# A graph layer with a mixture of experts: scatter the expert outputs to rows of their own and add them on TensorE, instead of accumulating them by DMA

## The chip, the cores and the metric

The kernel runs on one core of a Trainium2 chip. The metric is the device time of one execution in microseconds (us), the median of several runs. All data are float32 unless said.

## The reference, cut to what matters

```python
# x: 12500 x 256; src, dst: 212500 edges, sorted by dst; 64 experts, two for each node
h = x * rsqrt(deg_out)[:, None]
m = segment_sum(h[src], dst) * rsqrt(deg_in)[:, None]
x1 = (m @ W_gc + b_gc) + (x @ W_res + b_res)
vals, idx = top_k(x1 @ Wg + bg, 2);  gates = softmax(vals)
core = sum over a node's two experts e of  gate_e * (gelu(x1 @ w1[e] + b1[e]) @ w2[e] + b2[e])
y = x1 + core                                  # 256 -> 512 -> 256 in each expert
y = (y - mean over nodes) * rsqrt(var over nodes + eps) * gamma + beta
out = layernorm(x + y)                         # along the 256 features
```

The change touches how `core` of a part of the nodes is summed over the two experts of a node, and brought into `y`.

## The kernel before

**Nodes and stages.** The 12500 nodes are 98 tiles of 128 (the last has 84). Tiles 0 to 43 (`TA = 44`, 5632 nodes) are called the earlier nodes here, tiles 44 to 97 (6868 nodes) the later ones. By the trace, the stages are: loads and degrees, to 133 us; the edge stage, to about 2320, in which POOL gathers 128 rows of `h_d` at a time by indirect DMA (L766, 1596 of them) and PE sums them by destination with a one-hot matmul (L783), and in which the experts already work on the earlier nodes; some 30 us of tables; the expert stage for the later nodes, 2350 to 3032; the tail, which ends at 3163.

**The earlier nodes** have their experts' outputs in a DRAM tensor `oa_d`, in expert order. They are collected in the expert stage of the later nodes (below).

**The expert stage of the later nodes** (from L1675). The 64 experts come in descending order of their number of rows, each with room for a fixed number of rows (`TOKENS_B`, in units of 32), one part each: the first parts have four tiles of up to 128 rows, later ones two, the last ones one; 142 tiles in all. For each part:

- weights `w` and `bb` are loaded by SP (L1685, L1687), three buffers each;
- POOL gathers the part's node rows, one indirect DMA a tile, `xg` (L1695, 13 buffers), three parts ahead;
- PE transposes them (L1710), DVE copies them to `xT` (L1714);
- PE multiplies with the first weight (L1723), ACT applies gelu (L1727), PE multiplies with the second (L1750);
- DVE adds the bias and scales with the gate, into `yo` (L1755, L1760; 6 buffers);
- POOL scatters the 128 rows of `yo` by an indirect DMA to the DRAM tensor `z_d` (L1761), with `compute_op=ALU.add`: the DMA adds onto what the row holds. `z_d` has one row for each later node, and 1024 spare rows for empty slots.

A row of `z_d` gets two additions, from two experts. So `z_d` is zeroed ahead, by 31 DMAs of 256 KB on SP in the edge stage (L1629), and the scatters of different experts are ordered by semaphores: an expert's first scatter waits until the previous expert's last has landed. Scatters of one expert are declared independent (`group=f"expert{i}"`, "no node has an expert twice").

**Beside parts 0 to 43** one tile of the earlier nodes is collected a part: `brought` loads four tiles of `cy` from DRAM on SP (L1776) at every fourth part; `added` issues two gathers a tile on POOL from `oa_d` (`co`, L1785, 6 buffers), and DVE adds each with its gate onto `cy` (L1791); after each four, `turned_nodes` transposes them on PE (L1801), with `bn_stats` on DVE (L1802) and a copy on ACT (L1803) into `acc2`, which holds all nodes transposed (feature by node). The order on each engine is the order of the code: for part q the first matmuls, gathers for part q+3, transposes of part q+1, second matmuls and scatters of part q, then the collecting.

**The tail** (from L1913). SP loads `z_d` (L1926) into `zt`, in units of eight tiles (1 MB; the first has four, the last two one each), four buffers. `acc2` holds the later nodes' `x1` rows, not yet transposed. For the first four tiles of a unit DVE adds `zt` to them (L1930) and PE transposes the sum (L1943); for the other four PE transposes (L1945) and adds `zt` by a matmul with the identity that accumulates in the same PSUM (L1948). Then `bn_stats` on DVE (L1954) and a copy back on ACT (L1956). The first load waits for every scatter. Behind the loads, on SP, stands a prefetch of x (L1966, `z<-in_x`, six loads). When the last statistics are there, a short chain on DVE makes mean and variance over all nodes, and the final stage scales, transposes back (L2024, L2025), adds x, does the layer norm and stores.

Of the kernel before, what the change touches and what calls it, by code (L numbers as in the profile page):

```python
# [88 lines left out]
NA = TA * P  # L89
TOKENS_A = [  # L90
# [18 lines left out]
NODES_B = [(TA, 4)] + [(t, 8) for t in range(TA + 4, 96, 8)] + [(96, 1), (97, 1)]  # L109
# [30 lines left out]
def gnn_moe_kernel(  # L140
# [33 lines left out]
    z_d = dram.tile([NP - NA + 4 * 2 * P, D], F32, name="z_d")  # L174
# [1448 lines left out]
    z_all = z_d.rearrange("(a p r) d -> a p (r d)", p=P, r=2)  # L1623
    with tc.manual_schedule(engines=EVERY):
        fetch(0)
        for i in range(4):
            at_row(CA + 4 + 20 * i, lambda t, i=i: cleared([3 + i, NPW - 4 + i]))
        for i in range((NT - TA) // 2 + 4):
            at_row(CA + 90 + 12 * i, lambda t, i=i: nc.sync.dma_start(  # L1629
                z_all[i], acc_d[0][:, : 2 * D]  # L1630
            ))
        nodes_go[0] = True
        begin_nodes(CA)
        go(CA, MC)
# [10 lines left out]
    )  # L1645
    held = one.tile([P, NSLOT], F32)
# [11 lines left out]
    V.tensor_scalar_add(rank, rank, float(N - NA))  # L1658
    V.scalar_tensor_tensor(rank, held, 0.0, rank, op0=ALU.is_equal, op1=ALU.mult)
    V.tensor_tensor(slot[:, 1], rank, slot[:, 0], op=ALU.add)  # L1660
# [13 lines left out]
    with ExitStack() as stack:  # L1674
# [83 lines left out]
        def outputs(w, bb, at, gate, h1, m, group):  # L1758
            for k, r, yo in products(w, bb, h1, m):
                V.tensor_scalar_mul(yo[:r], yo[:r], gate[:r, k : k + 1])  # L1760
                st = GP.indirect_dma_start(  # L1761
                    out=z_d,
                    out_offset=bass.IndirectOffsetOnAxis(ap=at[:r, k : k + 1], axis=0),
                    in_=yo[:r],
                    in_offset=None,
                    compute_op=ALU.add,
                )
                if group:
                    tc.declare_no_dep(st.ins, group=group, reason="no node has an expert twice")
                    tc.add_to_no_dep_group(group, st.ins)  # L1770
# [79 lines left out]
        for q, (i, b, m) in enumerate(parts):  # L1850
            h1 = hidden(given[i][0], xT, m)
            if q + AHEAD < len(parts):
                begin(q + AHEAD)
            if q + 1 < len(parts):
                xT = turned(q + 1)
            outputs(*given[i], table(q, 1), gate.pop(q), h1, m, f"expert{i}")
            if q < TA:
                u, k = divmod(q, 4)
                if k == 0:
                    ys[u] = brought(u)  # L1860
                added(ys[u], pos_a[:, :, u * 4 : u * 4 + 4], k)
                if k == 3:
                    turned_nodes(ys[u], u)

        with tc.If(nc.values_load(over_n[0:1, 0:1]) > 0):
# [25 lines left out]
            for a in range(NT - TA):  # L1891
                nc.sync.dma_start(z_d[a * P : (a + 1) * P], none)
            with tc.For_i(0, E, 1) as e:
# [5 lines left out]
                for b in range(0, RPE, 4):  # L1899
                    g = gather(at[:, 0, b : b + 4], 4)  # L1900
                    gb = gates_of(g, second[:, b : b + 4])
                    outputs(w, bb, at[:, 1, b : b + 4], gb, hidden(w, turn(g), 4 * P), 4 * P, None)

    with ExitStack() as stack:
# [14 lines left out]
        z3 = z_d[: NP - NA].rearrange("(t p) d -> p t d", p=P)  # L1919
# [3 lines left out]
        for t0, n in [(t, n) for t, n in NODES_B]:  # L1923
            r = rows(t0)
            zt = zq.tile([P, 8, D], F32, name="zt")
            nc.sync.dma_start(zt[:r, :n], z3[:r, t0 - TA : t0 - TA + n])  # L1926

            m = min(n, 4)
            y = acc2[:r, :, t0 * P : (t0 + m) * P].rearrange("p h (t d) -> p t h d", d=P)
            V.tensor_add(y, y, zt[:r, :m].rearrange("p t (h d) -> p t h d", h=2))  # L1930
            if t0 == 96:
                continue
            for b in range(0, n, 4) if t0 < 96 else [-1]:
                for h in range(2):
                    q = ps2.tile([P, 4, P], F32, name="q")
                    at = 0
                    for i in range(4):
                        t = t0 + b + i
                        if t < NT:
                            r = rows(t)  # L1940
                            y = acc2[:r, h, t * P : (t + 1) * P]
                            if b < 4:
                                T.transpose(q[:, i, :r], y, ident[:r, :r])  # L1943
                            else:
                                T.matmul(  # L1945
                                    q[:, i], y, ident, start=True, stop=False, is_transpose=True
                                )
                                T.matmul(  # L1948
                                    q[:, i], zt[:, b + i, h * P : (h + 1) * P], ident,
                                    start=False, stop=True,  # L1950
                                )
                            at += r
                    q = q.rearrange("p a b -> p (a b)")[:, :at]
                    V.bn_stats(stat[:, h, (t0 + b) // 4], q)  # L1954

                    S.copy(acc2[:, h, (t0 + b) * P : (t0 + b) * P + at], q)  # L1956
# [148 lines left out]
```

## Time and profile before

| | us |
|---|---|
| median of 3 runs (lowest, highest) | 3160.55 (3154.66, 3164.33) |
| the profiled execution, its span | 3165.16, 3163.4 |
| busy in the span: PE, DVE, POOL, ACT | 2501.8, 1645.8, 2145.9, 728.5 |
| expert stage, parts 0 to 43 (2387 to 2860) | 473: PE busy 387.35, POOL 340.93 |
| last 16 scatters, from 2941 on | POOL busy 24.7 |
| PE's last expert matmul ends, first tail load | 3000.06, 3032.01 |
| first matmul of the final stage (L2024) | 3068.52 |

How to read it: PE is TensorE's matmuls and PEld its weight loads, DVE VectorE, ACT ScalarE, POOL GpSimd, SP SyncE (only DMA issues here). In the groups a row is line, engine, operation, out<-in, count, then busy time and mean ns of one, then the idle time just before them with what ended it. In the timelines a row is start, duration, engine, line, operation, and in brackets the idle time before it and its releaser. "issue" is time in which the engine waited for nothing that the profile shows. Releasers are inferred: where the engine that is named had long been done, it was something else. The granted clock of TensorE is 1.00 at full speed.

### The profile page before, as it was taken

The page shows a single profiled execution, that of the slowest core. Times are in us where ns is not written, and L with a number is a line of the kernel's source. Part 1 is how long each engine was busy: PE and PEld are TensorE (multiplying, and loading weights), DVE is VectorE, ACT ScalarE, POOL GpSimd, SP SyncE. Part 2 cuts the span into 40 slices and gives each one's busy share as a digit, 9 for nine tenths or more (in the row PEclk, how much of TensorE's full clock was granted, in tenths as well). Part 3 has the DMA queues.
Part 4 walks back from the last instruction along what each step waited for, and adds up shares of the span by engine and source line. Part 5 has one row for each costly group of instructions (what it writes and reads, how often), then busy time and mean ns, then how long its engine had stood idle before and what let it go on. Part 6 is the DMA issues. An engine that isn't in the chain of part 4 may idle for free. (4 is left out here: it accounts for less than half of the span.)

```text
span 3163.4 us, 41525 instructions
## 1 busy us (share of the span) xinstructions
PE 2501.8 (79%) x12664; PEld 1847.1 (58%) x12733; DVE 1645.8 (52%) x6067; ACT 728.5 (23%) x2126; POOL 2145.9 (68%) x2113
## 2 busy tenths in 40 slices
PE   2477777778788887898999989898958988679755
PEld 1244445544565654766777667677735666567655
DVE  8477765552487774553444343344554433334257
ACT  2022333330111111222221122122201112112246
POOL 0677777777777777777777777777747767666200
PEclk9889988996899998999999999999979999889878
DMA  8733333333665555666667677778746767778658
GB/s 285 241 96 101 102 105 104 109 114 113 207 182 164 159 164 162 184 187 189 198 193 207 201 207 209 204 232 256 230 128 154 179 174 197 182 205 227 203 156 269
DMA packets 297179, 567.59 MB, mean 179 GB/s; under 512 B 56921, under 2 KB 203493, under 8 KB 288753
## 3 DMA queue, kind: packets, MB, share of 16 engines
q0 software_dynamic: 110912, 271.07, 32.3%
q1 hardware_dynamic: 172325, 280.68, 28.4%
q10 hardware_dynamic: 13708, 13.06, 1.3%
q8 instruction: 105, 1.72, 0.2%
q14 instruction: 129, 1.06, 0.1%
HBM read 496.86 MB, written 75.89 MB: 181 GB/s over the span
## 5 line engine op out<-in xcount | busy, mean ns | idle before, releaser
L766 POOL DMA_INDIRECT ring<-h_d,src_col x1596 | 1575.6, 987 | 577.4 <-issue 427.8
L783 PE MATMUL p<-ring,o 128*128 128x257 f32 (+1 forms) x3192 | 1061.0, 434 | 316.4 <-DMA ring<-h_d,src_col 281.3
L783 PEld LDWEIGHTS p<-ring,o 128*128 128x128 f32 x3192 | 565.5, 205 | 548.7 <-DMA ring<-h_d,src_col 337.7
L758 DVE TENSOR_SCALAR o<-lane,rel 128x128 f32<-128x128 f32 x1596 | 399.7, 297 | 230.1 <-PE p L783 229.1
L1761 POOL DMA_INDIRECT z_d<-yo,tables x142 | 222.1, 1564 | 158.7 <-DVE yo L1755 65.2
L1750 PE MATMUL yp<-w,h 128*128 128x256 f32 (+3 forms) x1136 | 273.5, 392 | 39.0 <-DVE yo L1755 39.0
L1282 ACT ACTIVATE acc<-p,acc 128x128 f32<-128x128 f32 (+4 forms) x332 | 128.1, 386 | 736.0 <-PE p L1271 445.1
L236 DVE TENSOR_TENSOR acc<-bank,acc 125x2450 bf16<-125x2450 bf16 (+1 forms) x136 | 185.1, 1361 | 198.5 <-PE bank L1458 189.5
L1723 PE MATMUL hp<-xT,w 128*128 128x128 f32 (+12 forms) x1024 | 239.5, 389 | 60.4 <-DVE xT L1714 59.8
L1306 DVE TENSOR_TENSOR acc<-yp_a,acc 128x256 f32<-128x256 f32 (+3 forms) x120 | 50.1, 418 | 420.3 <-PE yp_a L1299 417.2
L1750 PEld LDWEIGHTS yp<-w,h 128*128 128x128 f32 (+3 forms) x1136 | 193.6, 178 | 96.7 <-DVE yo L1755 44.7
L1723 PEld LDWEIGHTS hp<-xT,w 128*128 128x128 f32 x1024 | 181.1, 205 | 112.2 <-DVE xT L1714 63.8
L1271 PE MATMUL p<-acc 128*128 128x128 f32 (+4 forms) x1328 | 238.0, 302 | 4.4 <-ACT s L818 0.6
L1271 PEld LDWEIGHTS p<-acc 128*128 128x128 f32 x1328 | 209.3, 193 | 47.1 <-ACT acc L1282 25.7
L1299 PE MATMUL yp_a<-acc 128*128 128x256 f32 (+3 forms) x960 | 235.6, 390 | 0.0
L1727 ACT ACTIVATE h<-hp,w 128x128 f32<-128x128 f32 (+12 forms) x256 | 117.0, 459 | 480.9 <-PE hp L1723 419.8
L1453 ACT ACTIVATE acc<-lane_b,acc 125x128 bf16<-125x128 bf16 x544 | 168.2, 389 | 240.8 <-PE bank L1462 149.5
L1299 PEld LDWEIGHTS yp_a<-acc 128*128 128x128 f32 (+3 forms) x960 | 162.9, 174 | 47.4 <-issue 9.6
L1695 POOL DMA_INDIRECT xg<-xb_d,tables x142 | 139.8, 985 | 44.3 <-issue 21.9
L818 ACT COPY s<-p 128x257 f32<-128x257 f32 (+1 forms) x133 | 49.6, 373 | 502.3 <-PE p L783 402.1
L1458 PEld LDWEIGHTS <-acc 125*128 125x128 bf16 x1156 | 88.4, 106 | 105.2 <-issue 62.5
L1235 POOL DMA_INDIRECT acc<-xa_d,tables x120 | 116.9, 974 | 36.5 <-issue 30.5
(349 smaller groups left out, 3122.6 us busy)
## 6 DMA issues: line engine op xcount, KB each, us to landing
w<-in_wpack SPq DMA_DIRECT2D x64, 1026.0 KB
acc<-in_wpack SPq DMA_DIRECT2D x128, 512.0 KB
ring<-h_d,src_col POOLq DMA_INDIRECT x1596
tables<-h_d SPq DMA_DIRECT2D x105, 128.0 KB
acc<-acc_d SPq DMA_DIRECT2D x14, 896.0 KB
xt<-in_x ACTq DMA_DIRECT2D x48, 256.0 KB
z<-in_x SPq DMA_DIRECT2D x12, 1024.0 KB
out<-z SPq DMA_DIRECT2D x11, 1024.0 KB
```

Source lines behind the costliest of these rows:

```text
L236: V.tensor_tensor(o.rearrange("p k (a b) -> p k a b", b=2), lane_b[:p, None, :n] .rearrange("p k (a b) -> p k a b", b=2) .to_broadcast([p, ...
L758: o_last[u] = V.tensor_scalar(o_of[u][:, j], lane, rel[:, c : c + 1], None, op0=ALU.is_equal)
L766: i = GP.indirect_dma_start(out=r[:, k, :D], out_offset=None, in_=h_d, in_offset=bass.IndirectOffsetOnAxis(ap=src_col[:, c : c + 1], axis=0),)
L783: i = T.matmul(p_of[g][:, :n], o_of[v][:, m], r[:, k, :n], start=j == 0, stop=j == GR - 1)
L1271: T.matmul(hp, w1[:, c, j * P : (j + 1) * P], xT[:, c, :m], start=c == 0, stop=c == 1,)
L1282: S.activation(h1[:, j, :m], hp_of.pop((q, j)), AF.Gelu, bias=b1_a[i % 2][:, j : j + 1])
L1299: T.matmul(y, h1[:, j, k * P : k * P + n], w2[:, j], start=j == 0, stop=j == 3)
L1453: S.activation(s_los[k % 2][:, j], lane_b[:EP], AF.Sign, bias=nbs[u % 2][:, i, j : j + 1])
L1695: GP.indirect_dma_start(out=g, out_offset=None, in_=of, in_offset=bass.IndirectOffsetOnAxis(ap=at[:, k : k + 1], axis=0),)
L1723: T.matmul(hp[:, :m], w1[:, c, j * P : (j + 1) * P], xT[:, c, :m], start=c == 0, stop=c == 1,)
L1750: T.matmul(yp[:r], h1[:, j, k * P : k * P + r], w2[:, j], start=j == 0, stop=j == 3,)
L1761: st = GP.indirect_dma_start(out=z_d, out_offset=bass.IndirectOffsetOnAxis(ap=at[:r, k : k + 1], axis=0), in_=yo[:r], in_offset=None, comp ...
```

## The change

`z_d` gets two planes of `ZR = NP - NA` rows, one for a node's first expert and one for its second (`second` is 1 where the slot holds the node's second expert), and behind them one spare row for every slot that can be empty. No row is written twice, so the scatter writes plainly, nothing is zeroed, and all scatters are in one group without dependences. In the tail each unit is four tiles, loaded from both planes by two DMAs of 512 KB; PE transposes the `x1` rows and accumulates both planes by two matmuls with the identity. Only the last two tiles are added on DVE.

```diff
+ZR = NP - NA
-NODES_B = [(TA, 4)] + [(t, 8) for t in range(TA + 4, 96, 8)] + [(96, 1), (97, 1)]
+NODES_B = [(t, 4) for t in range(TA, 96, 4)] + [(96, 1), (97, 1)]
-    z_d = dram.tile([NP - NA + 4 * 2 * P, D], F32, name="z_d")
+    z_d = dram.tile([2 * ZR + E * CAP, D], F32, name="z_d")
-        for i in range((NT - TA) // 2 + 4):
-            at_row(CA + 90 + 12 * i, lambda t, i=i: nc.sync.dma_start(
-                z_all[i], acc_d[0][:, : 2 * D]
-            ))
+    to = one.tile([P, NSLOT], F32)
+    GP.iota(
+        to, pattern=[[CAP, E], [P, RPE]], base=2 * ZR, channel_multiplier=1,
+        allow_small_or_imprecise_dtypes=True,
+    )
-    V.tensor_scalar_add(rank, rank, float(N - NA))
-    V.scalar_tensor_tensor(rank, held, 0.0, rank, op0=ALU.is_equal, op1=ALU.mult)
-    V.tensor_tensor(slot[:, 1], rank, slot[:, 0], op=ALU.add)
+    V.scalar_tensor_tensor(to, held, 0.0, to, op0=ALU.is_equal, op1=ALU.mult)
+    V.scalar_tensor_tensor(to, second, float(ZR), to, op0=ALU.mult, op1=ALU.add)
+    V.tensor_tensor(slot[:, 1], to, slot[:, 0], op=ALU.add)
...
                     in_=yo[:r],
                     in_offset=None,
-                    compute_op=ALU.add,
                 )
-                if group:
-                    tc.declare_no_dep(st.ins, group=group, reason="no node has an expert twice")
-                    tc.add_to_no_dep_group(group, st.ins)
+                tc.declare_no_dep(st.ins, group="z", reason="a row of its own for each output")
+                tc.add_to_no_dep_group("z", st.ins)
...
+        z4 = z_d[: 2 * ZR].rearrange("(k t p) d -> p k t d", p=P, k=2)
...
+            zt = zq.tile([P, 2, 4, D], F32, name="zt")
+            for k in range(2):
+                nc.sync.dma_start(zt[:r, k, :n], z4[:r, k, t0 - TA : t0 - TA + n])
+            if n == 1:
+                y = acc2[:r, :, t0 * P : (t0 + 1) * P]
+                for k in range(2):
+                    V.tensor_add(y, y, zt[:r, k, 0].rearrange("p (h d) -> p h d", h=2))
...
+                    else:
+                        T.matmul(q[:, i], y, ident, start=True, stop=False, is_transpose=True)
+                        for k in range(2):
+                            T.matmul(
+                                q[:, i], zt[:, k, i, h * P : (h + 1) * P], ident,
+                                start=False, stop=k == 1,
+                            )
```

On POOL, at the end of the expert stage, the last scatters with what each waits for (a DMASW name is the semaphore of one of eight slots for POOL's DMAs; a wait on its own slot is a matter of counting, the second one is the previous expert's last scatter). Before:

```order
L1761 DMA z_d<-yo,tables 7936x256 [waits DMASW3_49,DVE_49] x2
L1761 DMA z_d<-yo,tables 7936x256 [waits DMASW5_49,DVE_49]
L1761 DMA z_d<-yo,tables 7936x256 [waits DMASW6_49,DMASW5_49,DVE_49]
L1761 DMA z_d<-yo,tables 7936x256 [waits DMASW7_49,DMASW6_49,DVE_49]
L1761 DMA z_d<-yo,tables 7936x256 [waits DMASW7_49,DVE_49]
L1761 DMA z_d<-yo,tables 7936x256 [waits DMASW1_49,DMASW0_49,DVE_49]
```

The same place in the changed kernel:

```order
L1762 DMA z_d<-yo,tables 79360x256 [waits DMASW2_49,DVE_49]
L1762 DMA z_d<-yo,tables 79360x256 [waits DMASW3_49,DVE_49]
L1762 DMA z_d<-yo,tables 79360x256 [waits DMASW4_49,DVE_49]
L1762 DMA z_d<-yo,tables 79360x256 [waits DMASW5_49,DVE_49]
L1762 DMA z_d<-yo,tables 79360x256 [waits DMASW6_49,DVE_49]
```

The wait on the scatter just before is gone; what is left is the slot, which the DMA eight places earlier has used, and the `yo` from DVE. The order of the instructions on POOL, DVE and ACT is otherwise the same in this stage.

On SP, in the tail, the loads of z (`zt`) and the prefetch of x (`z<-in_x`). Before:

```order
L1926 DMA zt<-z_d 128x4x256
L1926 DMA zt<-z_d 128x8x256 x6
L1926 DMA zt<-z_d 128x256
L1966 DMA z<-in_x 128x8x256
L1926 DMA zt<-z_d 84x256
L1966 DMA z<-in_x 128x256
L1966 DMA z<-in_x 84x256
L1966 DMA z<-in_x 128x8x256 x3
```

The same place in the changed kernel, behind the first 14 loads of z:

```order
L1965 DMA z<-in_x 128x8x256
L1926 DMA zt<-z_d 128x4x256 x4
L1965 DMA z<-in_x 128x256
L1926 DMA zt<-z_d 128x4x256 x2
L1965 DMA z<-in_x 84x256
L1965 DMA z<-in_x 128x8x256
L1926 DMA zt<-z_d 128x4x256 x4
L1965 DMA z<-in_x 128x8x256
L1926 DMA zt<-z_d 128x4x256 x2
L1926 DMA zt<-z_d 128x256 x2
L1965 DMA z<-in_x 128x8x256
L1926 DMA zt<-z_d 84x256 x2
```

All six loads of x now stand ahead of the last z load; before, one did.

More of the change, by code (lines that the diff above doesn't have):

```diff
@@ L1621, in cleared @@
             )
-    z_all = z_d.rearrange("(a p r) d -> a p (r d)", p=P, r=2)
     with tc.manual_schedule(engines=EVERY):
@@ L1756, in products, with outputs @@
                 yield k, r, yo
-        def outputs(w, bb, at, gate, h1, m, group):
+        def outputs(w, bb, at, gate, h1, m):
             for k, r, yo in products(w, bb, h1, m):
@@ L1855, in gnn_moe_kernel @@
                 xT = turned(q + 1)
-            outputs(*given[i], table(q, 1), gate.pop(q), h1, m, f"expert{i}")
+            outputs(*given[i], table(q, 1), gate.pop(q), h1, m)
             if q < TA:
@@ L1890, in gnn_moe_kernel @@
                 turned_nodes(y, u)
-            for a in range(NT - TA):
+            for a in range(2 * (NT - TA)):
                 nc.sync.dma_start(z_d[a * P : (a + 1) * P], none)
@@ L1901, in gnn_moe_kernel @@
                     gb = gates_of(g, second[:, b : b + 4])
-                    outputs(w, bb, at[:, 1, b : b + 4], gb, hidden(w, turn(g), 4 * P), 4 * P, None)
+                    outputs(w, bb, at[:, 1, b : b + 4], gb, hidden(w, turn(g), 4 * P), 4 * P)
     with ExitStack() as stack:
@@ L1916, in gnn_moe_kernel @@
         nc.sync.dma_start(bet, beta.rearrange("(h p) -> p h", p=P))
-        z3 = z_d[: NP - NA].rearrange("(t p) d -> p t d", p=P)
+        z4 = z_d[: 2 * ZR].rearrange("(k t p) d -> p k t d", p=P, k=2)
         root_of = one.tile([P, 1], F32)
         S.activation(root_of, ones_f[:, 0:1], AF.Sqrt)
-        for t0, n in [(t, n) for t, n in NODES_B]:
+        for t0, n in NODES_B:
             r = rows(t0)
[L1925 to L1956, printed above, removed]
@@ new lines, in gnn_moe_kernel @@
+            zt = zq.tile([P, 2, 4, D], F32, name="zt")
[5 more added lines that the diff above has]
+                    V.tensor_add(y, y, zt[:r, k, 0].rearrange("p (h d) -> p h d", h=2))
+                if t0 == 96:
+                    continue
+                t0 = 96
+            for h in range(2):
+                q = ps2.tile([P, 4, P], F32, name="q")
+                at = 0
+                for i in range(min(4, NT - t0)):
+                    t = t0 + i
+                    r = rows(t)
+                    y = acc2[:r, h, t * P : (t + 1) * P]
+                    if n == 1:
+                        T.transpose(q[:, i, :r], y, ident[:r, :r])
+                    else:
[5 more added lines that the diff above has]
+                            )
+                    at += r
+                q = q.rearrange("p a b -> p (a b)")[:, :at]
+                V.bn_stats(stat[:, h, t0 // 4], q)
+                S.copy(acc2[:, h, t0 * P : t0 * P + at], q)
```

## Prediction

> **What bounds the kernel now.** I read the page first for the span, then a table by windows over the stages that the change touches, then in each stage the groups and the waits, and last the timelines around the stalls. The page gives:
>
> ```profile
> span 3163.4 us, 41525 instructions
> ```
>
> The profiled execution took 3165.16 us, 1.8 more than its span, and the median of the three timed runs is 3160.55, 4.6 below it. I sum against the span's rows and take the sum off the median. A difference under 0.3%, 9.5 us, is no change here.
>
> The windows (columns: length; busy us of PE, PEld, DVE, ACT, POOL with counts; granted clock of PE; DMA share; GB/s) are a piece of the edge stage with the zeroing in it, the expert stage in three pieces, the drain of the scatters, and the tail's loads:
>
> ```profile
> 910.00:1410.00 500.00, 424.58 (x1872) 300.96 (x1898) 329.56 (x1617) 80.37 (x273) 381.23 (x390) 0.95 0.59 170
> 2387.00:2860.00 473.00, 387.35 (x1724) 296.66 (x1723) 180.48 (x516) 86.66 (x176) 340.93 (x284) 0.91 0.71 184
> 2860.00:2941.00 81.00, 81.00 (x459) 62.73 (x457) 32.64 (x84) 21.06 (x53) 54.03 (x44) 1.00 0.88 240
> 2941.00:3000.00 59.00, 47.74 (x285) 42.69 (x283) 14.12 (x40) 16.16 (x44) 14.01 (x10) 0.88 0.68 203
> 3000.00:3032.00 32.00, 0.06 (x1) 0.00 (x0) 0.78 (x2) 1.49 (x2) 9.36 (x6) 0.54 0.27 30
> 3036.00:3068.00 32.00, 25.08 (x204) 24.48 (x204) 28.53 (x53) 15.91 (x29) 0.00 (x0) 0.87 1.03 329
> ```
>
> The edge stage is POOL's: 390 instructions of 381 us, with the 0.3 us that stands between any two (rows below), are 498 of 500 us. From 2860 to 2941 PE is busy all the time. From 3000 to 3032 nothing works but six scatters, one after another. The first window of the expert stage, 473 us, has no full engine: PE lacks 85.7 us, POOL 132. Who waits there (total us, times, longest):
>
> ```profile
> DVE cy L1791 <- DMA co<-oa_d,pos_a: 90.8, 20, 13.4
> PE hp L1723 <- DVE xT L1714: 47.4, 4, 14.3
> PE yp L1750 <- DVE yo L1755: 38.1, 12, 13.0
> DVE cy L1791 <- DMA cy<-xa_d: 24.4, 7, 6.8
> POOL z_d L1761 <- DMA z_d<-yo,tables: 10.5, 5, 3.8
> ```
>
> PE waits for DVE; DVE, which works in order, stands at an addition (L1791) whose gathered rows `co` have not come; and `co` is late because POOL issues it late. POOL's timeline shows why:
>
> ```profile
> 2699.93 1.58 POOL L1761 DMA_INDIRECT z_d<-yo,tables  x1 [0.30 <-issue]
> ...
> 2704.43 0.96 POOL L1785 DMA_INDIRECT co<-oa_d,pos_a  x1 [0.30 <-issue]
> 2707.71 1.62 POOL L1761 DMA_INDIRECT z_d<-yo,tables  x1 [2.32 <-DMA z_d<-yo,tables]
> 2709.64 0.99 POOL L1785 DMA_INDIRECT co<-oa_d,pos_a  x1 [0.30 <-issue]
> ```
>
> The scatter at 2707.71 is an expert's first. It waits for the landing of the previous expert's last, whose issue ended at 2701.51: 6.2 us. The gathers behind it stand meanwhile. On PE the result is a stall of 12.83 us and, behind it, a cold clock (the same 16 matmuls take 5.97 and, warm, 3.19 us):
>
> ```profile
> 2713.72 5.97 PE L1723 MATMUL hp<-xT,w 128*128 128x224 f32 x16 [12.83 <-DVE xT L1714]
> 2723.42 3.19 PE L1723 MATMUL hp<-xT,w 128*128 128x224 f32 x16
> ```
>
> **First window of the expert stage (473 us).** Removed: the wait between experts, and the add of the scatter. Moved: nothing; the order of POOL, DVE and ACT stays. POOL's groups there, with busy time, mean ns and idle time before:
>
> ```profile
> L1761 POOL DMA_INDIRECT z_d<-yo,tables x105 | 166.0, 1580 | 74.6 <-DVE yo L1755 22.1 <-issue 18.4 <-DVE gate L1737 11.6
> L1695 POOL DMA_INDIRECT xg<-xb_d,tables x100 | 98.6, 986 | 31.4 <-issue 14.3 <-PE yp L1750 7.9 <-PE xtp L1710 4.9
> ```
>
> A plain scatter on POOL is not in the trace. Its bounds are the scatter with add, 1.58, and the plain gather of as many rows, 0.986; I take the gather, as both are plain copies, so 0.594 us less each. PE's stalls, whose long ones are:
>
> ```profile
> 2409.03 5.16 PE L1750 MATMUL yp<-w,h 128*128 128x256 f32 x16 [12.97 <-DVE yo L1755]
> 2566.48 6.73 PE L1750 MATMUL yp<-w,h 128*128 128x256 f32 x16 [4.52 <-DVE yo L1755]
> 2618.91 2.56 PE L1750 MATMUL yp<-w,h 128*128 128x256 f32 x8 [3.31 <-DVE yo L1755]
> 2666.95 2.80 PE L1750 MATMUL yp<-w,h 128*128 128x256 f32 x8 [3.33 <-DVE yo L1755]
> 2759.67 5.20 PE L1723 MATMUL hp<-xT,w 128*128 128x224 f32 x16 [14.33 <-DVE xT L1714]
> 2799.96 5.53 PE L1723 MATMUL hp<-xT,w 128*128 128x224 f32 x16 [9.45 <-DVE xT L1714]
> 2841.72 4.70 PE L1723 MATMUL hp<-xT,w 128*128 128x192 f32 x16 [10.79 <-DVE xT L1714]
> ```
>
> - The four stalls of 47.4 us come once in four parts. In four parts POOL has eight scatters, 8 x 0.594 = 4.8 us, and its share of the landing waits, 10.5 / 4 = 2.6. So each shrinks by about 7.4: 30 us.
> - The stalls of 4.52, 3.31 and 3.33 are shorter than that and go: 11 us.
> - The first, 12.97, is the stage's start, before POOL is behind: 2 us.
> - The rest of the 38.1, about 13 us, falls on loads of `cy` by SP and stays.
> - Cold clock: behind a long stall the matmuls lose up to 5.97 - 3.19 = 2.8 us, and next to nothing behind the stall of 3.33. The stall of 4.52 goes, and those of 9.45 and 10.79 come down to 2 and 3.4: three times about 2.4, 7 us.
>
> Together 50 us. Below: if the scatter stays at 1.58, only the landing waits and the three short stalls go, 10.5 + 11 = 21. Above: POOL's sum becomes 340.9 - 62 + 284 x 0.3 = 364, below PE's own, so PE sets the floor: 387 busy, less some 20 of cold excess, plus 13 and 11 of stalls that stay, 391: a gain of 82.
>
> **Second window:** PE is full, 0.
>
> **Third window (59 us).** Here experts have one tile, and each scatter waits for the one before, so `yo` buffers run out and PE stops. PE is busy 47.74 of 59, so 11.3 us are stalls, and 1.8 us twice is cold clock (3.78 against 1.95):
>
> ```profile
> 2973.34 3.78 PE L1723 MATMUL hp<-xT,w 128*128 128x128 f32 x16 [4.64 <-DVE xT L1714]
> 2996.39 1.95 PE L1723 MATMUL hp<-xT,w 128*128 128x128 f32 x16
> ```
>
> That is 15; I take 13 (8 to 15), since the same weights must come in less time: 59 x 203 = 12.0 MB in 46 us is 260 GB/s, under the 329 that the tail shows.
>
> **The drain (32 us).** The last scatters go one after another, each waiting about 3 us for the one before; this is the last:
>
> ```profile
> 3026.56 1.55 POOL L1761 DMA_INDIRECT z_d<-yo,tables  x1 [3.01 <-DMA z_d<-yo,tables]
> ```
>
> After, only the last scatter stands behind PE's last matmul: DVE 0.8 (its busy time in the drain's window), POOL 1.0 to 1.6, and landing with SP's wake-up at most 3.9 (from 3028.11 to the tail's first load at 3032.01, below). So 32 becomes about 6: gain 26 (25 to 27).
>
> **The tail (36.5 us, from its first load to the next stage's first matmul).** It loads 7.03 MB of z before and 14.07 after, and the 4.41 MB of x that it prefetches now stand ahead of the last z loads in SP's order: 18.5 MB at 329 GB/s are 56 us, and some 5 us of start. But PE's part grows more. Before, half of the tiles were added on DVE; now every tile and half has a transpose and two matmuls that accumulate.
>
> ```profile
> 3032.01 21.18 SPq L1926 DMA_DIRECT2D zt<-z_d  x8
> 3036.37 1.23 DVE L1930 TENSOR_TENSOR acc<-acc,zt 128x1024 f32<-128x1024 f32 x1 [32.62 <-DMA zt<-z_d]
> 3037.65 1.97 PE L1943 MATMUL q<-ident,acc 128*128 128x128 f32 x8 [37.59 <-DVE acc L1930]
> 3044.93 0.27 PE L1945 MATMUL q<-ident,acc 128*128 128x128 f32 x1
> 3045.04 0.39 PE L1948 MATMUL q<-ident,zt 128*128 128x128 f32 x2
> 3045.26 0.27 PE L1945 MATMUL q<-ident,acc 128*128 128x128 f32 x1
> 3068.52 0.76 PE L2024 MATMUL q<-d_amp,acc 128*128 128x128 f32 x2 [4.73 <-issue]
> ```
>
> One fp32 matmul is two instructions in the trace. A transpose with one matmul comes every 0.333 us (3044.93 to 3045.26), 0.111 for each of three instructions; with two matmuls it is five, 0.555. There are 13 units of 4 tiles and 2 halves, 104 such groups: 57.7 us. Ahead of them stand the first load, 4.4 us (3032.01 to 3036.37), and the second copy's 0.5 MB, 1.6 more; five transposes are done by then (-0.5); the cold start, as in the row at 3037.65, costs about 2; and from PE's last to the next stage's first matmul it is about 4.7, the row at 3068.52, with half a microsecond for the last tiles. Together 6.0 - 0.5 + 2 + 57.7 + 4.7 = 69.9: cost 33 (29 if the clock is warm at once, 42 if it averages the 0.87 of now: 57.7 / 0.87 = 66.3). The DMA's 61 hides beneath PE.
>
> By a rule of the Trainium skill (DMA: Bandwidth & Descriptors, Bandwidth, "Batch DMAs to ≥1 MiB for ≥75% of peak", with the fit of 2.0 us and bytes over 436 GB/s for each DMA in Anatomy of one DMA), halving the loads to 512 KB speaks against the change: each would take 3.2 us, 26 of them 83, and the tail some 110, so that the whole would come to about 3145. The rows above speak against such a sum while loads overlap, since by it before's own loads would fill over 50 us and they took 36.5.
>
> **The rest.** The zeroing, 8 MB by SP in the edge stage, goes: POOL is full there whatever the queues do, 0 (0 to 2). Of the tables, one DVE operation more on 128 x 512 lies on the path, like L1659's 0.68 us (POOL's row first, then DVE's):
>
> ```profile
> 2320.46 1.26 POOL L1642 IOTA rank<- 128x512 f32 x1 [8.29 <-PE p L783]
> ```
>
> ```profile
> 2345.72 0.68 DVE L1659 SCALAR_TENSOR_TENSOR rank<-held,rank 128x512 f32<-128x512 f32 x1
> ```
>
> The new iota on POOL, like L1642's 1.26 us, has from 2320 until DVE reads it at 2345: 0, or 1.26 without that cover. The final stage, from 3068.5 on, is unchanged.
>
> **Sum:** 50 + 0 + 13 + 26 - 33 - 0.7 = 55 us. A profiled run goes from 3165.2 to about 3110, the median from 3160.55 to 3105.
>
> **Rivals.**
> 1. The plain scatter is as dear on POOL as the add. For: POOL is the engine that is late in the first window, and no row prices a plain scatter. Gain 21 in place of 50: 3134. Chance 0.17.
> 2. The first window reaches PE's floor, 391 us. For: POOL's new sum of 364 leaves room to be ahead. Against: POOL's work is bunched, eight gathers in a row behind each long stall. Gain 82 in place of 50: 3073. Chance 0.14.
> 3. DVE's order holds the waits, not POOL: the stalls shift from one late `co` to the next. Then only the 10.5 us of landing waits, 5 of the third window and the drain are gained: 10.5 + 5 + 26 - 33 - 0.7 = 8, 3153, no change. For: 90.8 us of DVE's waits are for gathers, which stay. Chance 0.10.
> 4. Slower: the tail's loads, two to a unit and tied to its buffers, go one after another. The first load took 4.36 us from issue to its reader; 26 of those and six of x are 32 x 4.36 = 140, and 4.7 more: a tail of 144, cost 108 against gains of 88, 3180. It decides from a tail of 36.5 + 88 = 125 us on, that is when 18.5 MB come at under some 155 GB/s. Against: before's loads overlap, at 329 GB/s with four buffers, and four buffers remain, now eight loads. Chance 0.05. (The Trainium skill's 3.2 us a load, from the page above, is less than this row's 4.36 and gives the 3145 above.)
>
> **How the numbers follow.** My own case has 0.54, with 3085 to 3120 as its own range. Faster by over 0.3% are my case, 1 and 2: 0.85; case 3 is the same, 0.10; case 4 slower, 0.05. The range 3070 to 3142 holds my case and the first two, and takes in the bounds of the scatter's price (21 to 82) and of the tail (29 to 42) one at a time; 3 and 4 lie outside it, and a little of 1 and 2.
>
> **What would show it.** In the changed profile: scatters of about 1.0 us on POOL and no wait of a scatter for a scatter; the first window about 423 us long, with the stalls on `xT` down from 47 to some 17; the third about 46; about 6 us between PE's last expert matmul and the first z load; then a PE that is busy without gaps for some 58 us at 0.555 us for a transpose and two matmuls, with DMA at a lower rate than now. I am wrong if the scatter stays at 1.5 us or more, if PE in the tail stands waiting for `zt`, or if the stalls on `xT` and `yo` keep their length.

## The result and the profile after

The changed kernel takes 3071.74 us (median of 4 runs, 3070.61 to 3074.44); the kernel before, run beside it, 3157.61. The ratio is 0.9727, 95% interval 0.9707 to 0.9746: 86 us less, where 55 were forecast. The time lies in the range of 3070 to 3142, 1.7 us above its lower end, and below the 3085 to 3120 that the prediction gave as its own case.

The windows of the changed kernel, in the same order and columns as before: the expert stage in its three pieces (cut at the same matmuls), the drain, the tail, and the part of the tail in which PE adds.

```profile
2376.90:2777.60 400.70, 371.56 (x1724) 287.93 (x1723) 180.40 (x516) 86.85 (x177) 277.53 (x285) 0.98 0.69 217
2777.60:2858.60 81.00, 81.00 (x458) 62.73 (x457) 32.63 (x84) 21.10 (x53) 43.22 (x46) 1.00 0.75 242
2858.60:2901.30 42.70, 41.60 (x285) 37.99 (x283) 14.55 (x40) 16.18 (x44) 10.71 (x11) 1.00 0.84 292
2901.30:2906.98 5.68, 0.75 (x6) 0.53 (x5) 0.78 (x2) 1.49 (x2) 0.97 (x1) 0.96 0.14 33
2906.98:2976.60 69.62, 60.20 (x519) 60.04 (x520) 24.08 (x52) 15.92 (x29) 0.00 (x0) 0.92 0.83 266
2912.00:2971.00 59.00, 59.00 (x510) 59.00 (x511) 19.71 (x30) 14.66 (x25) 0.00 (x0) 0.96 0.92 295
```

The first window went from 473 to 401 us, the second stayed at 81, the third went from 59 to 43, the drain from 32 to 5.7, the tail from 36.5 to 69.6, and PE is busy without a gap for 59 us of it.

POOL's groups in the first window (busy time, mean ns, idle time before):

```profile
L1762 POOL DMA_INDIRECT z_d<-yo,tables x106 | 103.5, 977 | 38.3 <-issue 16.8 <-DVE yo L1761 8.6 <-DVE gate L1738 4.4
L1696 POOL DMA_INDIRECT xg<-xb_d,tables x100 | 96.7, 967 | 50.7 <-PE xtp L1711 24.5 <-issue 12.8 <-PE yp L1751 9.1
```

The plain scatter costs POOL 0.977 us, like the gather beside it; it was 1.580 with the add. In this stage no scatter is seen to wait for a scatter any more. POOL now waits for PE (24.5 us for `xtp`), where PE waited for POOL's work before. Who waits (total us, times, longest):

```profile
DVE cy L1790 <- DMA co<-oa_d,pos_a: 28.5, 20, 4.8
PE yp L1751 <- DVE yo L1756: 16.7, 8, 10.1
PE hp L1724 <- DVE xT L1715: 12.3, 4, 4.0
```

DVE's waits for `co` fell from 90.8 to 28.5 us. The long stalls of PE are these, with the first of the stage ahead:

```profile
2396.61 6.05 PE L1751 MATMUL yp<-w,h 128*128 128x256 f32 x16 [10.07 <-DVE yo L1756]
2661.56 3.29 PE L1724 MATMUL hp<-xT,w 128*128 128x224 f32 x16 [2.67 <-DVE xT L1715]
2693.84 4.98 PE L1724 MATMUL hp<-xT,w 128*128 128x224 f32 x16 [3.34 <-DVE xT L1715]
2726.76 3.29 PE L1724 MATMUL hp<-xT,w 128*128 128x224 f32 x16 [2.30 <-DVE xT L1715]
2759.53 4.55 PE L1724 MATMUL hp<-xT,w 128*128 128x192 f32 x16 [4.03 <-DVE xT L1715]
```

The four that were 12.83, 14.33, 9.45 and 10.79 us are 12.3 in all, and behind two of them the clock is no longer cold (3.29 us for the matmuls behind, against 5.97 behind the stall of 12.83).

Before the change the short stalls cost clock too. Around the one of 3.33 us, 8 matmuls of one shape took 1.89 us ahead of it and 2.80 behind it, and 16 of another 3.72 and 4.54; the granted clock from 2666.95 to 2674.00 was 0.76:

```profile
2657.73 3.72 PE L1723 MATMUL hp<-xT,w 128*128 128x256 f32 x16
2661.72 1.89 PE L1750 MATMUL yp<-w,h 128*128 128x256 f32 x8
2666.95 2.80 PE L1750 MATMUL yp<-w,h 128*128 128x256 f32 x8 [3.33 <-DVE yo L1755]
2669.54 4.54 PE L1723 MATMUL hp<-xT,w 128*128 128x256 f32 x16
```

The end of the expert stage and the tail: POOL's last two scatters, SP's first loads, then one group of the tail on PE and the first matmul of the final stage.

```profile
2898.14 0.97 POOL L1762 DMA_INDIRECT z_d<-yo,tables  x1 [2.76 <-DVE yo L1761]
2902.45 0.97 POOL L1762 DMA_INDIRECT z_d<-yo,tables  x1 [3.34 <-DVE yo L1761]
```

```profile
2906.98 7.16 SPq L1926 DMA_DIRECT2D zt<-z_d  x8
```

```profile
2963.88 0.61 PE L1947 MATMUL q<-ident,zt 128*128 128x128 f32 x4
2964.33 0.27 PE L1945 MATMUL q<-ident,acc 128*128 128x128 f32 x1
2964.44 0.61 PE L1947 MATMUL q<-ident,zt 128*128 128x128 f32 x4
2964.89 0.27 PE L1945 MATMUL q<-ident,acc 128*128 128x128 f32 x1
...
2976.61 0.77 PE L2023 MATMUL q<-d_amp,acc 128*128 128x128 f32 x2 [4.52 <-DVE base L1990]
```

A transpose with two matmuls comes every 0.56 us (2964.33 to 2964.89), forecast 0.555.

The account of the two profiled executions, in us of span: edge stage to the last gather +12.1, tables -2.0 (the first window starts 10.1 earlier), first window +72.3, second 0, third +16.3, drain +26.3, tail -33.1, final stage +1.8: 93.7, the difference of 3163.4 and 3069.7. The medians differ by 86 only, since the profiled execution of before, 3165.16 us, was longer than each of its timed runs.

### The profile page after: what moved, and what is told of

Same layout as the page of the kernel before. It is cut to its first block, busy times and chain, and to the rows that moved or that the text cites. A ratio compares the mean times of both kernels' runs of the same rounds, so it can differ in the third digit from the quotient of the medians.

```text
span 3069.7 us, 42189 instructions
## 1 busy us (share of the span) xinstructions
PE 2510.7 (82%) x12984; PEld 1867.0 (61%) x13053; DVE 1644.5 (54%) x6062; ACT 729.5 (24%) x2126; POOL 2048.1 (67%) x2114
## 3 DMA queue, kind: packets, MB, share of 16 engines
q14 instruction: 129, 1.06, 0.1%
## 5 line engine op out<-in xcount | busy, mean ns | idle before, releaser
L1751 PE MATMUL yp<-w,h 128*128 128x256 f32 (+3 forms) x1136 | 263.9, 383 | 17.8 <-DVE yo L1756 17.8
L1724 PE MATMUL hp<-xT,w 128*128 128x128 f32 (+12 forms) x1024 | 227.2, 374 | 15.2 <-DVE xT L1715 14.1
L1724 PEld LDWEIGHTS hp<-xT,w 128*128 128x128 f32 x1024 | 171.4, 194 | 63.0 <-issue 25.3
L1762 POOL DMA_INDIRECT z_d<-yo,tables x142 | 137.8, 971 | 94.0 <-DVE gate L1738 37.6
```

What stands on the lines that cost most here:

```text
L1724: T.matmul(hp[:, :m], w1[:, c, j * P : (j + 1) * P], xT[:, c, :m], start=c == 0, stop=c == 1,)
L1751: T.matmul(yp[:r], h1[:, j, k * P : k * P + r], w2[:, j], start=j == 0, stop=j == 3,)
L1762: st = GP.indirect_dma_start(out=z_d, out_offset=bass.IndirectOffsetOnAxis(ap=at[:r, k : k + 1], axis=0), in_=yo[:r], in_offset=None,)
```

## The experiments

The theory: in the expert stage two things count together, the price of a scatter on POOL and its wait for the previous expert; in the drain only the wait; in the tail PE's matmuls. Rivals: the wait alone, or the price alone; a tail that is set by the bytes of z.

### The changed kernel again

> The changed kernel once more, as the yardstick for the runs beside it: 3072 us, and a ratio to the kernel before of 0.973. If the 12 us by which its edge stage was shorter than that of the profiled kernel before (2312.2 against 2300.1 us at the last gather) are the change's doing, the last gather starts near 2299 again; if they belong to that one execution of the kernel before, the ratio alone says so: 0.973 leaves 86 us of which the expert stage, the drain and the tail account for 72 + 16 + 26 - 33 = 81.

3068.46 us, ratio 0.9715 (0.9682 to 0.9748). Its last gather starts at 2293.8 us, the first window takes 401.8. So the shorter edge stage is not an accident of one execution; a second execution of the kernel before, further down, agrees (last gather at 2310.8).

### The scatter adds, nothing waits

```diff
-    z_d = dram.tile([2 * ZR + E * CAP, D], F32, name="z_d")
+    z_d = dram.tile([2 * ZR + E * P, D], F32, name="z_d")
+        for i in range((2 * ZR + E * P) // 256):
+            at_row(CA + 90 + 4 * i, lambda t, i=i: nc.sync.dma_start(z_all[i], ...))
                     in_=yo[:r],
                     in_offset=None,
+                    compute_op=ALU.add,
```

> Rows of their own and no wait between experts, but the scatter adds (onto rows that 86 DMAs on SP zero in the edge stage; the spare rows are 8192 in place of 65536). Theory (both parts of the scatter count: its price on POOL where POOL is late, its wait where it stands in a chain): the scatter costs POOL 1.55 us, POOL's sum in the first window of the expert stage is about 340 busy + 85 of issue gaps = 426, and the window takes 425 to 445 in place of 401; the third window (43) and the drain (6) stay short, within 2 us. In all 3095 to 3120. Rival, only the wait counts: 3072 to 3080, first window near 401. Rival, only the price counts: first window back near 473, in all 3140 or more.

3112.15 us, 44 above the changed kernel on the same chip. Its windows (first, third, drain) and POOL's scatter in the first:

```profile
2382.80:2816.30 433.50, 378.93 (x1724) 292.45 (x1723) 179.30 (x516) 86.66 (x176) 340.17 (x285) 0.95 0.76 200
2897.20:2939.00 41.80, 41.22 (x285) 38.29 (x283) 14.55 (x41) 16.16 (x44) 17.10 (x11) 1.00 0.96 303
2939.00:2945.70 6.70, 1.30 (x5) 0.93 (x5) 0.77 (x2) 1.49 (x2) 1.55 (x1) 0.68 0.38 44
```

```profile
L1767 POOL DMA_INDIRECT z_d<-yo,tables x106 | 165.1, 1557 | 35.2 <-issue 20.1 <-DVE yo L1766 5.9 <-DVE yo L1761 2.4
```

The scatter is back at 1.557 us on POOL, and the first window at 433.5, as the sum 426 of POOL foretold; third window and drain stay short. So the add is worth some 32 us of the first window (433.5 against 401.8), and nothing in the third window; the drain takes 1 us more. Another 13 us lie in the edge stage: the last gather starts at 2306.8.

### Plain scatters that wait for the previous expert

```diff
-                tc.declare_no_dep(st.ins, group="z", reason="a row of its own for each output")
-                tc.add_to_no_dep_group("z", st.ins)
+                if group:
+                    tc.declare_no_dep(st.ins, group=group, reason="a row of its own for each output")
+                    tc.add_to_no_dep_group(group, st.ins)
...
-            outputs(*given[i], table(q, 1), gate.pop(q), h1, m)
+            outputs(*given[i], table(q, 1), gate.pop(q), h1, m, f"expert{i}")
```

> The changed kernel with the wait between experts put back: a plain scatter, but an expert's first waits for the last one of the expert before. Theory (both count): a plain scatter lands in some 3 to 4 us, so that a part's chain of two scatters and one landing is about 6 us, under the 7 of PE's part: the first window takes 401 to 420. In the third window one scatter and its landing, 1.0 + 3 us, are about PE's 3.7 us a part: 43 to 50; the drain 6 to 12. In all 3075 to 3105. Rival, only the wait counts: first window near 460, third near 55, in all 3140 or more. Rival, only the price on POOL counts: nothing changes, 3072.

3099.19 us, 31 above. Windows, and POOL in the drain:

```profile
2372.90:2792.70 419.80, 373.52 (x1723) 289.87 (x1722) 179.78 (x516) 86.67 (x176) 276.84 (x285) 0.96 0.64 206
2873.60:2915.70 42.10, 41.58 (x285) 38.13 (x283) 14.54 (x40) 16.17 (x44) 7.12 (x8) 1.00 0.81 287
2915.70:2934.74 19.04, 1.30 (x5) 0.93 (x5) 0.78 (x2) 1.49 (x2) 4.85 (x5) 0.59 0.13 41
```

```profile
2927.10 0.97 POOL L1762 DMA_INDIRECT z_d<-yo,tables  x1 [2.19 <-DMA z_d<-yo,tables]
2930.25 0.97 POOL L1762 DMA_INDIRECT z_d<-yo,tables  x1 [2.18 <-DMA z_d<-yo,tables]
```

The wait alone costs 18 us in the first window and 13 in the drain, which is 19 and not the 6 to 12 expected: by PE's end five scatters are still to be issued, one every 3.15 us (4.55 with the add). In the third window it costs nothing (42.1, where 43 to 50 were expected). Before the change, the first window was 473; without the add it is 420, without the wait 434, without either 401. Each part alone gains more than is left for it once the other is gone: both act on the same lateness of POOL. Neither rival holds there. In the drain the two go together as well: without the wait it is 5.7 us, and 6.7 with an add; with the wait it is 19 for a plain scatter and 32 for one that adds, since each scatter then stands until the one before has landed.

### The zeroing put back

```diff
+        for i in range((NT - TA) // 2 + 4):
+            at_row(CA + 90 + 12 * i, lambda t, i=i: nc.sync.dma_start(z_all[i], acc_d[0][:, : 2 * D]))
```

> The changed kernel with the 31 zeroing DMAs of 256 KB put back into the edge stage. Theory (POOL is full there): 3072, within 3 us, and the last gather starts within 2 us of the run without them. Rival (the zeroing took DMA time from the gathers): 8 to 12 us more, all between 900 and 1400 us.

3071.69 us (3067.62 to 3075.54) against 3068.46 (3066.33 to 3069.0) beside it; the last gather starts at 2295.5 (2293.8 without). The zeroing is hidden, as forecast: 3.2 us in all, under the rival's 8 to 12. The edge stage's 12 us come from elsewhere (last experiment).

### The tail: half of z's bytes, one matmul in place of two, larger loads, DVE

These four ran on another chip, on which the kernel before takes 3794 us. In these four most of the extra time is in the edge stage, whose last gather starts at 2925 to 2948 us. It is mainly their tails that are read here, from the first load to the final stage's first matmul; the changed kernel's is 69.6 us (70.0 in its other two profiles).

One plane loaded and added twice (the second plane is left out, but for the last two tiles):

```diff
-            for k in range(2):
+            for k in range(2 if n == 1 else 1):
                 nc.sync.dma_start(zt[:r, k, :n], z4[:r, k, t0 - TA : t0 - TA + n])
...
-                                q[:, i], zt[:, k, i, h * P : (h + 1) * P], ident,
+                                q[:, i], zt[:, 0, i, h * P : (h + 1) * P], ident,
```

> The changed kernel, whose tail loads only the first plane of z_d (except for the last two tiles) and adds it twice, so the second plane is left out: half of z's bytes, all of PE's work. From the first tail load to the first matmul of the final stage the changed kernel takes 69.6 us, in which PE is busy 59 us without a gap. Theory (PE sets the tail): 66 to 70, and PE again full for 58 to 59 us. Rival (the bytes set it): 11.5 MB as before the change, 37 to 45.

One matmul (the second plane is left out of the sum, but for the last two tiles):

```diff
-                        for k in range(2):
+                        for k in range(1):
                             T.matmul(
```

> The changed kernel, whose tail loads both planes but adds only the first by a matmul (the second plane is left out of the sum, except for the last two tiles): all bytes, PE's work 104 x 0.333 = 35 us in place of 58. Theory (PE sets the tail, and DMA is the next bound): 18.5 MB at about 345 GB/s are 54 us, with start and statistics 60 to 64 in place of 69.6. Rival (the bytes set it already): 69 to 70.

Pairs:

```diff
-    V.scalar_tensor_tensor(to, second, float(ZR), to, op0=ALU.mult, op1=ALU.add)
-    V.tensor_tensor(slot[:, 1], to, slot[:, 0], op=ALU.add)
+    V.scalar_tensor_tensor(to, second, 1.0, to, op0=ALU.mult, op1=ALU.add)
+    V.scalar_tensor_tensor(slot[:, 1], slot[:, 0], 2.0, to, op0=ALU.mult, op1=ALU.add)
...
-            for k in range(2):
-                nc.sync.dma_start(zt[:r, k, :n], z4[:r, k, t0 - TA : t0 - TA + n])
+            nc.sync.dma_start(zt[:r, :n], z4[:r, t0 - TA : t0 - TA + n])
```

> The changed kernel with a node's two rows side by side in z_d (row = 2 x node + second), so a unit is one load of 1 MB with 2 KB pieces in place of two of 512 KB with 1 KB pieces. Theory (PE sets the tail, the size of a load does not matter): the tail stays at 69 to 71, within 2 us. Rival (small loads hold it up): 60 to 66.

DVE in 7 units:

```diff
+            dve = n == 4 and (t0 // 4) % 2 == 1
+            if dve:
+                V.tensor_add(zt[:, 0], zt[:, 0], zt[:, 1])
...
-                        for k in range(2):
+                        for k in range(1 if dve else 2):
```

> The changed kernel, in which DVE adds the two planes of 7 of the 13 units, so that these need one matmul in place of two; nothing is left out. PE: 7 x 2.66 + 6 x 4.44 = 45 us. Theory: DMA is the next bound, 60 to 64 us of tail in place of 69.6, and 3062 to 3066 in all, 6 to 9 less than the changed kernel beside it. Rival (the bytes set the tail already): 69 to 71, no gain.

The tails of the four, in this order:

```profile
3643.86:3713.05 69.19, 59.78 (x519) 59.63 (x520) 24.05 (x52) 15.91 (x29) 0.00 (x0) 0.92 0.56 170
```

```profile
3616.66:3668.26 51.60, 39.11 (x311) 36.37 (x312) 23.90 (x52) 16.07 (x29) 0.00 (x0) 0.90 1.06 331
```

```profile
3615.60:3687.05 71.45, 60.22 (x519) 60.07 (x520) 24.10 (x52) 15.90 (x29) 0.00 (x0) 0.91 0.74 260
```

```profile
3622.62:3683.23 60.61, 47.31 (x407) 46.90 (x408) 31.46 (x59) 15.93 (x29) 0.00 (x0) 0.89 0.97 306
```

With half of z's bytes the tail stays (69.2, and PE is full for 58 us of it); with one matmul less it falls to 51.6, and the DMA engines are full (share 1.06, 331 GB/s). So PE's matmuls set the tail, and the bytes come next. But the second run changed more than PE's work: on SP all of z's loads came first and all of x's behind them, issued from 39 us into the tail on, where the changed kernel issues the first of x after 21 us:

```profile
3616.66 39.00 SPq L1926 DMA_DIRECT2D zt<-z_d  x30
3655.70 9.78 SPq L1965 DMA_DIRECT2D z<-in_x  x6
```

That is why the expected 60 to 64 was too long: it counted x's 4.4 MB too, and here z's loads did not have to share with x, of which a part lands after the tail's end. How much of the 18 us comes from PE's work and how much from x's new place was not separated. In the changed kernel itself PE has no gap for 59 us, so there x's place cannot be what holds the tail. With DVE's help, where all but one of x's loads stand behind the first 28 of z, the tail is 60.6. Loads of 1 MB bring no gain (71.5, against 69.6 to 70.1 for the changed kernel on other chips).

In all, the kernel with DVE's help was 0.9947 (0.9916 to 0.9979) of the kernel before on that chip, and the pairs were at 0.9967 (0.9932 to 1.0003), an interval that includes no gain. The changed kernel itself was not run there, but both of these hold its scatters, so the change seems to gain far less on that chip. The first window of the expert stage takes 475 us there (with DVE's help), although the scatter costs 0.97 us. ACT waits 79 us of it for what the profile calls "remote", a wait that the changed kernel on the first chip does not show; what is behind it, and what the kernel before takes in each stage there, was not measured.

### Both kernels once more, and a version with a cheaper tail

On yet another chip, with profiles of both:

> The kernel before, once more with a profile, to set its stages beside those of the changed kernel on one chip: ratio 1.00. On a chip like the first: last gather 2295 to 2311 us, first window of the expert stage 465 to 475, third 59, drain 32, tail 36.5. The chip of the four tail runs was about a fifth slower in the edge stage, and the changed kernels gained only 0.3 to 1.0% there; on such a chip I expect the first window to be some 475 to 480 before the change too, since there something other than the scatters holds the engines; third window, drain and tail as above.

> The changed kernel beside it. On a chip like the first: 0.972 of before, first window 401, third 43, drain 5.7, tail 69.6. On a chip like that of the tail runs: 0.995 to 1.000, first window 470 to 478, the rest as above.

Before 3159.83 (1.0007 of the kernel before beside it), after 3072.84: ratio 0.972 (0.9704 to 0.9737), as on the first. First window, third window and drain of the kernel before:

```profile
2387.00:2862.60 475.60, 385.98 (x1723) 296.75 (x1722) 180.93 (x516) 86.66 (x176) 338.99 (x284) 0.91 0.70 182
2943.60:2989.25 45.65, 41.92 (x285) 37.95 (x283) 14.05 (x39) 16.16 (x44) 9.78 (x7) 1.00 0.80 259
2989.25:3022.08 32.83, 0.00 (x0) 0.00 (x0) 1.13 (x3) 1.49 (x2) 10.97 (x7) 0.53 0.26 30
```

The last gather starts 17.5 us earlier after the change (2293.3 against 2310.8). The first window is 77 us shorter after (398.8), the drain 27, the tail 32.5 longer; but the third window was 45.7 here before the change and is 42.2 after. So its gain is not steady: 16 us in one pair, 3.5 in the other.

The version: DVE adds the planes in all units, a node's rows are pairs as above, and SP issues in the order of the code, x behind all of z.

```diff
+        fixed = tc.manual_schedule(engines={SP})
+        fixed.__enter__()
...
+            dve = n == 4
+            if dve:
+                V.tensor_add(zt[:, :, 0], zt[:, :, 0], zt[:, :, 1])
-                        for k in range(2):
+                        for k in range(1 if dve else 2):
```

> A version against the tail's cost: DVE adds the two planes in every unit of four tiles, so PE has one matmul a tile and half (35 us in all); a node's rows lie side by side and a unit is one load of 1 MB; SP's order is fixed so that x comes behind all of z. Nothing is left out. Theory (with PE relieved, z's 14.1 MB at 345 GB/s are the bound, 41 us, and 4.4 of start, 3 for the last unit, 4.7 of statistics): tail 52 to 56 in place of 69.6, 14 to 18 us less than the changed kernel beside it (3054 on a chip like the first). Rival (x, which now comes late, is waited for in the final stage): the tail is as short, but the final stage, 93 us, is 8 to 13 longer, and the gain 2 to 8.

3060.40 us, ratio 0.9678 (0.9661 to 0.9694), 12.4 below the changed kernel beside it. Its tail:

```profile
2910.18:2966.45 56.27, 41.00 (x311) 37.42 (x312) 37.46 (x65) 15.93 (x29) 0.00 (x0) 0.86 0.90 310
```

56.3 against 70.0, at the long end of what was expected; the final stage takes 94.4 against 94.1 in the changed kernel beside it, and DVE waits for x 2.2 us there against 1.5, so the late x costs next to nothing. The gain of 12.4 is a little under the 14 to 18 expected. This version beats both kernels; which of its three parts gives how much was not separated.

### A scatter that adds in a branch that is not taken

```diff
-                    outputs(w, bb, at[:, 1, b : b + 4], gb, hidden(w, turn(g), 4 * P), 4 * P)
+                    outputs(w, bb, at[:, 1, b : b + 4], gb, hidden(w, turn(g), 4 * P), 4 * P, ALU.add)
```

> The changed kernel, in which only the scatters of the fallback branch (L1886 and on, not taken with these data) add; those that run are plain as before. In the edge stage the gather of h_d takes POOL at least 949 ns (median 953 to 957) in the three programs whose scatters add, and at least 942 (median 946 to 949) in the plain ones, and the last gather starts at 2307 to 2311 against 2293 to 2302 us. Theory (it hangs on the program holding such a scatter, run or not): at least 949 ns here, the last gather near 2307 or later, the whole 8 to 14 us above the changed kernel, 3080 to 3086. Rival (it hangs on the scatters that run, by what the execution before left behind): 942 ns, 2293 to 2302, 3068 to 3073.

3070.53 us, ratio 0.975 (0.9726 to 0.9773). The gather of the edge stage (ns: least, median, most), in the kernel before, the changed one, the adding one and this one:

```profile
L766 POOL DMA_INDIRECT ring<-h_d,src_col x1596: 950/957/3973, 97.2 to 2311.2; - x200
```

```profile
L767 POOL DMA_INDIRECT ring<-h_d,src_col x1596: 942/949/3977, 97.4 to 2299.1; - x200
```

```profile
L767 POOL DMA_INDIRECT ring<-h_d,src_col x1596: 949/953/3979, 97.5 to 2306.8; - x200
```

```profile
L767 POOL DMA_INDIRECT ring<-h_d,src_col x1596: 942/946/3977, 97.1 to 2293.8; - x200
```

The theory falls: that the program holds such a scatter is not enough. All three profiles of kernels whose running scatters add show at least 949 or 950 ns, each of the eleven of a plain one 940 to 942; the medians differ by 7 to 8 ns between an adding and a plain kernel on one chip, and times 1596 gathers that is 11 to 13 us. But this does not show that the running adds are the cause, for the size of `z_d` went along with them: it has 7936 rows in the kernel before and 22016 in the adding run, and 79360 in every run with plain scatters. A plain scatter with a small `z_d` was not run. The zeroing is not the cause, since it is in the run with 941 ns at least ("The zeroing put back"). Why a gather in the edge stage, which comes before any scatter of its execution, should feel either stays open.

## Why the prediction was right or wrong

- **The whole.** The parts of the sum that were named came out in sign, and most of them in size. The gain beyond the forecast, 31 us by the medians and 39 by the two profiled spans, lies mainly in two places: 22 in the first window and 12 in the edge stage (17.5 in the second pair). The range held the time by 1.7 us only, and without the edge stage in its sum; that it held is in part luck.
- **First window: right in the mechanism, too small.** Forecast 50, measured 72 (77 in the second pair). The four long stalls shrank by 35 us (30 forecast), the other stalls of PE from 38.1 to 16.7 (13 forecast, since I let 13 us of stalls on loads of `cy` stay; they halved), and PE's busy time for the same matmuls fell from 387.35 to 371.56, with the granted clock up from 0.91 to 0.98: 15.8 us of cold clock where I had 7. The terms mis-sized are the cold clock and the short stalls. That the matmuls lose "next to nothing behind the stall of 3.33" misread the row: it says 2.80 us, against 1.89 for the same matmuls ahead of it, and the 16 matmuls after it take 4.54, against 3.72. The matmuls right behind the four long stalls gave back 5.3 us, so the larger part of the 15.8 lies elsewhere, as behind the short ones. The price of the plain scatter, taken from the gather, was right (0.977 against 0.986).
- **Second window:** 0, as forecast.
- **Third window:** 13 forecast, 16 and 3.5 measured; the forecast rested on one execution of a stage that varies, so the first pair came near it partly by luck. The reason given, the wait for the scatter before, does not lengthen this window alone (42.1), nor does the add alone (41.8); only kernels with both showed more.
- **Drain:** 26 forecast, 26.3 measured. Taking only the wait away gives 25 of it (6.7 us left with adds); taking only the add away gives 13 (19 left).
- **Tail:** a cost of 33 forecast, 33.1 measured, with PE full at 0.56 us a group; that PE and not the bytes sets it is shown by half of z's bytes, which leave the tail as long. The run with one matmul less fits this, though x moved in it too.
- **Edge stage: wrong.** "POOL is full there whatever the queues do, 0". The zeroing indeed costs nothing; but POOL being full, 7 to 8 ns less for a gather are worth 11 to 13 us. I priced what was removed and nothing that could change the gathers beside it; no row of before showed it. Whether it hangs on the scatter's kind or on the size of `z_d` is open.
- **Tables:** 0.7 us forecast; the time from the last gather to the first scatter is 76.0 and 76.1 before, 77.8, 76.3 and 75.9 after, so it does not show.
- **Rivals.** The time of the second (3073) came true, but not its sum: the first window is at 401 and not at PE's floor of 391, and the rest is the edge stage. The first, a scatter as dear as the add, is refuted by the row, and what the add is worth was measured: 32 us. The third, waits that DVE's order holds, fell, since DVE's waits for `co` went from 90.8 to 28.5. The fourth, loads one after another, fell: 348 GB/s in the tail's full slices. The Trainium skill's rule (DMA: Bandwidth & Descriptors, Bandwidth) to batch DMAs to 1 MiB or more for 75% of peak made no difference here, as loads of 1 MB, 71.5 us of tail, are no better than those of 512 KB while PE is the bound. The fit that the prediction took beside it from the Trainium skill (DMA: Bandwidth & Descriptors, Anatomy of one DMA) is given there for DMAs that GpSimd issues; these loads are issued by SP, and all 26 came within a tail of 69.6 us, where that fit gave 83 for them.

## What to carry to other kernels

In this kernel a scatter that accumulates costs three times: on the issuing engine (1.58 against 0.98 us), in the wait for its landing (3.0 against 2.2 us in the drain), and in the order that it needs; rows of one's own trade that for bytes and adds later, so count which engine does the later adds before choosing it. Where an engine is late, a price and a wait on it overlap: what each is worth alone (53 and 39 us here) does not add up to what both are worth (72). Fewer stalls also give back the cold clock behind them, here 16 us, a fifth of the first window's gain.

## What the runs showed that was not expected

- A gather on POOL takes 940 to 942 ns at least in the runs with plain scatters and a `z_d` of 79360 rows, and 949 to 950 in those with adding scatters and a smaller `z_d`, even in a stage before any scatter (above); on a full POOL that is about 12 us.
- Chips differ: on one, the kernel before takes 3794 us in place of 3158, and the two versions of the changed kernel that leave nothing out only 0.3 and 0.5% less, the first of them within its interval of no gain.
- With pieces of 2 KB the tail's loads ran at up to 408 GB/s, with pieces of 1 KB at about 348 for most of the tail (slices of the DMA view below: the changed kernel, then the version with the cheaper tail, whose last slices are x, in pieces of 1 KB). In the run with one matmul less, where PE does not hold the loads back, most slices stand at 346 to 350 too.

```profile
GB/s 36 291 364 348 348 348 348 343 346 249 275 327 71 381 353 347 346 339 356 304 210 374 304 355 345 347 352 348 348 350 346 347 344 151 21 0 0 0 0 0
```

```profile
GB/s 14 246 338 344 363 408 399 386 383 133 165 344 395 389 382 377 310 386 255 309 350 171 399 329 385 373 399 301 335 375 209 1 119 224 345 347 312 350 348 348
```
